# Attention in a macaron block: the maxima of pairs 0 and 1 in one loop on four row groups, pair 0 two steps at a time, projections in single matmuls among the maxima

## The chip, the cores and the metric

The kernel runs on one core of one Trainium2 chip. The core has a matrix engine (TensorE, "PE" in the profile, with its weight loads "PEld"), three engines that work on 128 partitions (VectorE "DVE", ScalarE "ACT", GpSimd "POOL"), and queues for transfers, of which SyncE ("SP") issues those of this kernel. TensorE writes only into PSUM, [...]the other engines empty it. The metric is the device time of one launch in microseconds (us): 3159.78 us, the median of three runs of the kernel before (3156.42 to 3159.99).

## The reference

The block computes, for 2048 tokens x of width 512, three residual stages:

```
x = x + 0.5 * FFN(layernorm(x))
x = x + attention(layernorm(x))      # 16 heads of width 32, causal
x = x + 0.5 * FFN(layernorm(x))      # 4096 hidden, gelu(gate) * up, 4-bit weights dequantized

scores = q @ k.T / sqrt(32);  attn = softmax(scores + causal mask);  out = attn @ v
```

All of it is fp32. Only the middle stage is changed.

## The kernel before, in words

The program is one list of instructions per engine, in the order in which the Python code issues them; each engine works through its list and waits for semaphores where an operand isn't there or a buffer isn't free. So the order of the code is the order of TensorE's queue.

**Tiles.** Tokens are worked on in 16 tiles of 128 (NT) and 4 blocks of 512 (NB). xT[tb] is the normed and transposed input of a block. A projection of q and k (project_qk(u), line 1115) makes 128 rows, four heads, that is two *pairs* of heads: pieces of 4 matmuls (k = 0..3), one for each block and for q and k, into qT and kT, with the bias added on the way out of PSUM. Heads are 32 wide, so a head's q and k are one *row group* of 32 of TensorE's 128 rows; matmuls on different row groups run at once. Pair p uses the row groups 2(p % 2) and 2(p % 2)+1 (quadrant). project_v(half) makes v of 8 heads for two token tiles in a piece, in vals. wqk_sb holds the weights of one u and is refilled by SP.

**Maxima and attention.** For each pair, maxima(p) (lines 1206 to 1243) makes scores with queries on the partitions, q tile by k block, pm; VectorE reduces each to a column (with the mask for a diagonal block, lines 1214 and 1218). There are 40 steps, of two heads each, in blocks g of 4, 8, 12 and 16 steps (STARTS). At the end of a block, finish() splits the maxima into three bf16 pieces on GpSimd, and a few steps later rows() transposes them on TensorE and copies them to mrow (lines 1242 and 1243). attend(p) makes scores anew with keys on the partitions, ps: first a matmul with ones that puts the negated maximum of each query under it (line 1357), then k by q (line 1366); ScalarE takes the exponential into pt (line 1391). A diagonal step masks a 128x128 part first: head 0 with an add on VectorE (line 1381), head 1 by a copy on ScalarE (1384), a select on GpSimd (1385) and an exponential of its own (1393). Then columns() (line 1278) multiplies v and, for the denominators, ones with pt or with the sum of two of them (lines 1413 to 1415). At the end of a block the result is divided: for all pairs but the last through small transfers that spread the denominators over partitions, take the reciprocal and bring it back (flat, packs, back); for the last one directly, a 128x128 reciprocal on VectorE and 32x128 products on GpSimd (chunk).

**Order.** First four pieces of q and k, with the norms of blocks 2 and 3 between them, two steps of norms per maxima step after that. Then maxima(0) alone with 12 whole pieces (the rest of q and k, and v) as fills; then for each pair attend(p) interleaved with maxima(p + 1), so that four row groups are busy in every pass: two with ps, two with pm. The last pair has no maxima ahead and takes two steps at a time; for this the other half of its row groups gets a copy of q and k. Projections of later pairs are fills in the diagonal steps (plan, after_step). Norms are of class Norm (lines 83 to 170): the moments by VectorE's bn_stats and a square root on ScalarE, or, with moments_on_act and power, by sums and squares on ScalarE (lines 99 and 105) and a power on GpSimd (lines 121 to 131).

**Buffers.** PSUM: seven single banks in rotation (ps_one), for pm, ps, rows, projections and transposes, and one for the sums of attention (ps_acc). pt has four buffers, sums two.

## Time and profile before

| what | us |
|---|---|
| median of three runs | 3159.78 |
| the profiled run | 3161.12 |
| its span on the core | 3159.3 |
| first q/k and norms, 1193.9 to 1209.6 | 15.7 |
| maxima of pair 0 alone, 1209.6 to 1291.0 | 81.4 |
| pair 0 with the maxima of pair 1, to 1391.5 | 100.5 |
| pair 1 with the maxima of pair 2, to 1467.6 | 76.1 |
| pair 7, 1959.3 to 2037.7 | 78.4 |

Stages are taken from the first matmul of line 1357 of each pair. In the views, times are from the start of the span; a line of a timeline is start, duration, engine, source line, operation, output and inputs with their shapes, and how many in a row; a bracket gives the idle time of the engine ahead of it and what ended it. A line of the stage table is a stretch, its length, and the busy time and the number of instructions of each engine, then the granted clock of TensorE as a share of the full one, the busy share of the DMA engines and GB/s.

### The profile page before, as it was taken

To read this page: it belongs to the slowest core of one execution; us is meant where nothing else is said; L and a number is where in the kernel's file an instruction comes from. 1 tells how busy PE (TensorE), PEld (TensorE's weight loads), DVE (VectorE), ACT (ScalarE), POOL (GpSimd) and SP (SyncE) were. 2 spreads that over 40 slices of the span, in tenths; PEclk is the share of its full clock that TensorE was granted. 3 is DMA by queue.
4 is the path that set the end of the run, shared out by engine and by line. 5 is a ranking of instruction groups with operands and counts; after the bars stand their busy time and mean duration, and the time that the engine had idled before them with its cause. 6 is when DMAs were issued, how large, how long until landed. Compare 5 with 4: busy or idle time off the path is not lost.

```text
span 3159.3 us, 45153 instructions
## 1 busy us (share of the span) xinstructions
PE 3114.4 (99%) x16592; PEld 2006.8 (64%) x16592; DVE 2055.9 (65%) x3182; ACT 1047.2 (33%) x2070; POOL 1534.8 (49%) x1529
## 2 busy tenths in 40 slices
PE   7999999999999999999999999999999999999998
PEld 4556565656565565444335434478888878888887
DVE  6666666666666655655564566687666777666775
ACT  5111111111111122355453456443333343333332
POOL 3767675857667672456564467522232223223221
PEclk9999999999999999999999999999999999999999
DMA  3223122212122220000000000064444445344441
GB/s 140 79 85 114 67 97 90 97 60 97 64 93 80 83 87 24 5 14 9 12 9 7 29 20 11 1 203 130 124 127 129 125 131 171 116 124 129 130 122 61
DMA packets 261293, 260.21 MB, mean 82 GB/s; under 512 B 21216, under 2 KB 225616, under 8 KB 257104
## 3 DMA queue, kind: packets, MB, share of 16 engines
q1 hardware_dynamic: 261072, 257.33, 25.0%
q8 instruction: 131, 2.15, 0.3%
q14 instruction: 90, 0.74, 0.1%
HBM read 176.28 MB, written 79.92 MB: 81 GB/s over the span
## 4 chain that ended last, share of the span: by engine, by line
PE 93%; DVE 2%; ACT 1%; POOL 1%; issue 1%; DMA 1%; SPq 0%; ACTq 0%; POOLq 0%; DVEq 0%
PE po L438 12%; PE d_f L746 12%; PE pg L339 12%; PE pu L339 12%; PE av L1278 7%; PE pod_f L877 7%; PE pm L1206 6%; PE f_f L746 6%; PE pqk L1122 4%; PE pof_f L877 3%; PE e_f L746 3%; PE ps L1357 2%; PE pv L1139 2%; PE pp L1159 2%; PE poe_f L877 2%; PE ps L1366 1%
## 5 line engine op out<-in xcount | busy, mean ns | idle before, releaser
L1391 ACT ACTIVATE pt<-ps 128x512 f32<-128x512 f32 (+3 forms) x608 | 288.2, 528 | 180.8 <-PE ps L1366 118.5
L1206 PE MATMUL pm<-kT,qT 32*128 32x512 f32 (+3 forms) x1280 | 332.3, 572 | 0.0
L1218 DVE TENSOR_REDUCE parts<-pm 128x1 f32<-128x512 f32 x384 | 246.6, 686 | 129.3 <-PE pm L1206 128.9
L746 PE MATMUL d_f<-ys_f,ring 128*128 128x256 f32 x1216 | 319.8, 384 | 10.1 <-DVE o_f L779 5.8
L1415 POOL TENSOR_TENSOR sum<-pt,pt 128x512 f32<-128x512 f32 (+1 forms) x225 | 265.9, 1202 | 95.2 <-ACT pt L1391 88.1
L1366 PE MATMUL ps<-qT,kT 32*128 32x512 f32 (+3 forms) x1280 | 278.3, 536 | 0.0
L746 PEld LDWEIGHTS d_f<-ys_f,ring 128*128 128x128 f32 x1216 | 226.4, 190 | 58.2 <-DVE o_f L779 21.3
L438 PEld LDWEIGHTS po<-wd,inter 128*128 128x128 f32 x1024 | 194.4, 190 | 77.5 <-issue 55.7
L800 DVE TENSOR_TENSOR o_f<-o_f,o_f 128x1024 f32<-128x1024 f32 x128 | 203.6, 1601 | 61.2 <-ACT o_f L785 56.5
L438 PE MATMUL po<-wd,inter 128*128 128x256 f32 x1024 | 241.1, 379 | 0.0
L339 PE MATMUL pg<-xT_f,w 128*128 128x512 f32 x512 | 240.6, 598 | 0.0
L339 PE MATMUL pu<-xT_f,w 128*128 128x512 f32 x512 | 238.0, 592 | 0.0
L892 POOL TENSOR_TENSOR xq<-xq,d_f 128x512 f32<-128x512 f32 x48 | 63.7, 1326 | 314.6 <-DVE xq L886 229.4
L452 POOL TENSOR_TENSOR xq<-xq,d 128x512 f32<-128x512 f32 x124 | 161.8, 1315 | 92.5 <-DVE xq L446 56.2
L892 POOL TENSOR_TENSOR xq_second<-xq_second,d_f 128x512 f32<-128x512 f32 x45 | 61.6, 1370 | 279.6 <-DVE xq_second L886 210.9
L1278 PE MATMUL av<-pt,vals 128*32 128x256 f32 (+1 forms) x2432 | 191.5, 369 | 2.4 <-ACT both L1300 2.3
L393 POOL TENSOR_TENSOR u<-u,u 128x512 f32<-128x512 f32 x64 | 81.9, 1279 | 211.1 <-ACT u L390 210.4
L438 PEld LDWEIGHTS po<-wd,s 128*128 128x128 f32 x768 | 145.5, 190 | 57.9 <-issue 39.2
L438 PE MATMUL po<-wd,s 128*128 128x256 f32 x768 | 181.4, 379 | 0.0
L339 PE MATMUL pg<-xsum,w 128*128 128x512 f32 x384 | 179.6, 597 | 0.0
L800 POOL TENSOR_TENSOR o_f<-o_f,o_f 128x1024 f32<-128x1024 f32 x44 | 119.2, 2709 | 123.8 <-ACT o_f L785 122.7
L339 PE MATMUL pu<-xsum,w 128*128 128x512 f32 x384 | 177.7, 592 | 0.0
(225 smaller groups left out, 6345.9 us busy)
## 6 DMA issues: line engine op xcount, KB each, us to landing
wd_f<-kept SPq DMA_DIRECT2D x112, 256.0 KB
kept<-wd SPq DMA_DIRECT2D x8, 1792.0 KB
xq<-in_x SPq DMA_DIRECT2D x16, 256.0 KB
pk<-in_gate_codes SPq DMA_DIRECT2D x16, 256.0 KB
sc<-in_gate_scales SPq DMA_DIRECT2D x32, 128.0 KB
pk<-in_up_codes SPq DMA_DIRECT2D x16, 256.0 KB
sc<-in_up_scales SPq DMA_DIRECT2D x32, 128.0 KB
pk<-in_down_codes SPq DMA_DIRECT2D x16, 256.0 KB
```

The lines of the kernel that those rows point to most:

```text
L339: nc.tensor.matmul(ps, lhsT=a[:, j, :], rhs=b[:, j, :], start=(j == 0), stop=(j == 1))
L438: nc.tensor.matmul(ps[:, j, :], lhsT=a[i][:, k, bass.ts(2 * q + j, P)], rhs=b[i][:, k, :], start=(k == 0), stop=(k == 1),)
L452: adder.tensor_tensor(dst, dst, other, ALU.add)
L746: nc.tensor.matmul(ps[:, k, :], lhsT=fa[k][y], rhs=fb[k][y], start=first and k == 0, stop=True, skip_group_check=True,)
L800: sums.append(lambda: eng.tensor_tensor(dst, dst, other, ALU.add))
L877: nc.tensor.matmul(ps[:, j, :], lhsT=a[:, k, bass.ts(2 * q + j, P)], rhs=wd[:, PLACE[i], k, :], start=new and j == k == 0, stop=True, skip ...
L1206: nc.tensor.matmul(ps[a][:, :n], lhsT=q[r, bass.ts(4 * g + i, P)], rhs=k[r, kb * 512 : kb * 512 + n], start=True, stop=True,)
L1218: nc.vector.tensor_reduce(most, scores, AX.X, ALU.max)
L1278: nc.tensor.matmul(dst_, lhsT=lhsT, rhs=rhs, start=kw.get("start", False), stop=True, skip_group_check=True)
L1366: nc.tensor.matmul(ps[a][:, off:], lhsT=k[r, bass.ts(c, P)], rhs=q[r, g * 512 + off : (g + 1) * 512], start=False, stop=True,)
L1391: nc.scalar.activation(pt[:, a, plain[a] :], ps[a][:, plain[a] :], AF.Exp, scale=scale)
L1415: eng.tensor_tensor(s[:, a, off_2:], one[:, a, off_2:], other[:, a, off_2:], ALU.add)
```

## The change

The pairs 0 and 7 form DOUBLE. The maxima of pairs 0 and 1 are made in one loop: each step issues the matmuls of both pairs (four row groups), then the four reductions. Pair 0 is then attended two steps at a time with no maxima beside it, as pair 7 is. Its second row groups read copies of q and k of rows 0 to 63, put into rows 64 to 127 of two tiles by SP, and a second copy of its maxima's rows (mcopy). The projections are cut into units, one matmul of q/k or two of v, issued three per step for three steps and then two per step; they now take in six of eight pieces of the second group of q and k (following), whose weights are fetched in mid-stage (second_group), and the other two are fills of pair 0. Even pieces of these use the bank of ps_acc until attend begins. Only two pieces of q/k go ahead of the maxima, and norms take three steps per maxima step; the norm of block 3 takes its moments on ScalarE and its power on GpSimd. The bias of the first half of v is added on GpSimd after a copy by ScalarE. In pairs 0 and 7 both heads of a diagonal step are masked on VectorE, the division is direct, and VectorE makes one half of the sums. In the diff, whose lines but the first few are all inside attention(), the indentation is cut by twelve.

```diff
...
 STARTS = (0, 4, 12, 24)
+DOUBLE = (0, NPAIR - 1)
 MASKED = -1e30
...
 qT = [qkp.tile([P, S], F32, tag=f"qT{i}", name=f"qT{i}") for i in range(2)]
 kT = [qkp.tile([P, S], F32, tag=f"kT{i}", name=f"kT{i}") for i in range(2)]
-split = [qkp.tile([P, 4, 64], BF16, tag=f"split{i}", name=f"split{i}") for i in range(2)]
+split = [qkp.tile([P, 4, 64], BF16, tag=f"split{i}", name=f"split{i}") for i in range(4)]
 for t in split:
...
 dens = [qkp.tile([P, 256], F32, tag=f"den{i}", name=f"den{i}") for i in range(2)]
...
 ones_f = aw.tile([P, HD], F32, tag="ones_f", name="ones_f")
 nc.gpsimd.memset(ones_f, 1.0)
+copies = [an.tile([P, S], F32, tag="attnT", name=f"copy{i}", bufs=3) for i in range(2)]
+mcopy = [an.tile([P, D], F32, tag="xn", name=f"mcopy{i}").bitcast(BF16) for i in range(2)]
 def normed(nm):
...
     xT.append(x_transposed("a", tb))
-    norms += Norm("a", tb, xT[tb], normed).steps()
-def project_qk(u):
+    norms += Norm("a", tb, xT[tb], normed, moments_on_act=tb == 3, power=tb == 3).steps()
+def joined(pieces):
+    def whole(units):
+        for f in units:
+            f()
+    return [lambda units=units: whole(units) for units in pieces]
+def project_qk(u, bank=None):
     w = wqk_sb
     def piece(tb, j):
-        ps = ps_one.tile([P, 512], F32, tag="one", name=f"pqk_{u}_{j}_{tb}")
-        for k in range(4):
-            nc.tensor.matmul(ps, lhsT=w[:, j, k, :], rhs=xT[tb][:, k, :], start=(k == 0), stop=(k == 3))
-        bias = bqk_sb[:, j, u : u + 1]
-        if j == 0 or u == 0:
-            nc.scalar.activation((qT, kT)[j][u % 2][:, bass.ts(tb, 512)], ps, AF.Identity, bias=bias)
-        else:
-            nc.vector.tensor_scalar(kT[u % 2][:, bass.ts(tb, 512)], ps, bias, None, ALU.add)
-    return [lambda tb=tb, j=j: piece(tb, j) for tb in range(NB) for j in range(2)]
-def project_v(half):
+        ps = []
+        def unit(k):
+            if k == 0:
+                pool, tag = bank(2 * tb + j) if bank else (ps_one, "one")
+                ps.append(pool.tile([P, 512], F32, tag=tag, name=f"pqk_{u}_{j}_{tb}"))
+            nc.tensor.matmul(
+                ps[0], lhsT=w[:, j, k, :], rhs=xT[tb][:, k, :], start=(k == 0), stop=(k == 3)
+            )
+            if k == 3:
+                bias = bqk_sb[:, j, u : u + 1]
+                if j == 0 or u < 2:
+                    nc.scalar.activation(
+                        (qT, kT)[j][u % 2][:, bass.ts(tb, 512)], ps[0], AF.Identity, bias=bias
+                    )
+                else:
+                    nc.vector.tensor_scalar(kT[u % 2][:, bass.ts(tb, 512)], ps[0], bias, None, ALU.add)
+        return [lambda k=k: unit(k) for k in range(4)]
+    return [piece(tb, j) for tb in range(NB) for j in range(2)]
+def project_v(half, bank=None):
     def piece(t2):
-        ps = ps_one.tile([P, 2, 256], F32, tag="one", name=f"pv_{half}_{t2}")
-        for i in range(2):
+        ps = []
+        def unit(n):
+            if n == 0:
+                pool, tag = bank(t2) if bank else (ps_one, "one")
+                ps.append(pool.tile([P, 2, 256], F32, tag=tag, name=f"pv_{half}_{t2}"))
+            i = n // 2
             t = 2 * t2 + i
-            for k in range(4):
+            for k in (2 * (n % 2), 2 * (n % 2) + 1):
                 nc.tensor.matmul(
-                    ps[:, i, :],
+                    ps[0][:, i, :],
                     lhsT=xT[t // 4][:, k, (t % 4) * P : (t % 4 + 1) * P],
...
                 )
-        for i in range(2):
-            nc.vector.tensor_tensor(
-                vals[:, 2 * t2 + i, :, :].rearrange("p h d -> p (h d)"), ps[:, i, :],
-                bv_sb[:, bass.ts(half, 256)], ALU.add,
-            )
-    return [lambda t2=t2: piece(t2) for t2 in range(NT // 2)]
+            if n < 3:
+                return
+            both = vals[:, 2 * t2 : 2 * t2 + 2, :, :].rearrange("p t h d -> p t (h d)")
+            if half == 0:
+                nc.scalar.copy(both, ps[0])
+            for i in range(2):
+                eng, src = (nc.gpsimd, both) if half == 0 else (nc.vector, ps[0])
+                eng.tensor_tensor(both[:, i, :], src[:, i, :], bv_sb[:, bass.ts(half, 256)], ALU.add)
+        return [lambda n=n: unit(n) for n in range(4)]
+    return [piece(t2) for t2 in range(NT // 2)]
 def project_out(u):
...
                 nc.vector.tensor_reduce(nmax, parts, AX.X, ALU.max, negate=True)
-                sp = split[g % 2]
+                sp = split[g % 2 + 2 * (p == 1)]
                 left = nmax
...
                     piece = sp.rearrange("p i (a c) -> p a i c", c=HD)[:, :, :, j]
...
                 def rows(g=g, sp=sp):
-                    halves = (p % 2,) if p + 1 < NPAIR else (0, 1)
+                    halves = (0, 1) if p in DOUBLE else (p % 2,)
                     h = slice(64 * halves[0], 64 * halves[-1] + 64)
...
                             nc.tensor.transpose(row[64 * i : 64 * i + 64, bass.ts(b, P)], sp[:, b, :], identb)
+                    if p == 0:
+                        nc.scalar.copy(mcopy[g // 2][64:, bass.ts(g % 2, 512)], row[64:, :])
+                        h = slice(0, 64)
                     nc.scalar.copy(mrow[h, bass.ts(g, 512)], row[h, :])
...
             rc = dens[g % 2]
-            direct = p == NPAIR - 1
+            direct = p in DOUBLE
             if not direct:
                 flat = store.tile([4, 256], F32, tag=f"flat{g % 2}", name=f"flat_{p}_{g}")
...
         i = 0 if copied else (p // 2) % 2
-        q, k = qT[i], kT[i]
+        q, k = (qT[i], kT[i]) if p or not copied else copies
         def rows_of(a):
-            return slice(HD * a, HD * a + HD) if copied else quadrant(p, a)
+            return quadrant(p + copied, a)
         def maxrows(a):
...
             ps[a] = ps_one.tile([P, 512], F32, tag="one", name=f"ps_{p}_{g}_{c}_{a}")
+            m, at_ = (mrow, g) if p or not copied else (mcopy[g // 2], g % 2)
             nc.tensor.matmul(
...
                 lhsT=ones_b[r.start : r.start + 3, :],
-                rhs=mrow[r.start : r.start + 3, g * 512 + off : (g + 1) * 512],
+                rhs=m[r.start : r.start + 3, at_ * 512 + off : (at_ + 1) * 512],
                 start=True, stop=False,
             )
...
             plain = [off, off]
             if c >= 4 * g:
-                plain[1] = off + P
-                own = pt[:, 1, off : off + P]
-                nc.vector.tensor_tensor(
-                    ps[0][:, off : off + P], ps[0][:, off : off + P], mask_k, ALU.add
-                )
-                nc.scalar.copy(own, ps[1][:, off : off + P])
-                nc.gpsimd.affine_select(
-                    out=own, in_=own, compare_op=ALU.is_ge, fill=MASKED, base=0,
-                    pattern=[[1, P]], channel_multiplier=-1,
-                )
+                for a in range(2 if p in DOUBLE else 1):
+                    own = ps[a][:, off : off + P]
+                    nc.vector.tensor_tensor(own, own, mask_k, ALU.add)
+                if p not in DOUBLE:
+                    plain[1] = off + P
+                    own = pt[:, 1, off : off + P]
+                    nc.scalar.copy(own, ps[1][:, off : off + P])
+                    nc.gpsimd.affine_select(
+                        out=own, in_=own, compare_op=ALU.is_ge, fill=MASKED, base=0,
+                        pattern=[[1, P]], channel_multiplier=-1,
+                    )
             for a in range(2):
...
                     nc.scalar.activation(pt[:, a, plain[a] :], ps[a][:, plain[a] :], AF.Exp, scale=scale)
...
                 else:
                     s = pp.tile([P, 2, 512], F32, tag="sum", name=f"sum_{p}_{g}_{n}", bufs=2)
-                    engines = (nc.vector if p + 1 == NPAIR else nc.gpsimd, nc.gpsimd)
+                    engines = (nc.vector if p in DOUBLE else nc.gpsimd, nc.gpsimd)
                     def add():
                         if off_1 < off_2:
...
         fill[1] -= 1
-qk, v = project_qk(0), project_v(0)
-for piece in qk[:4]:
+begun = []
+def bank(n):
+    return (ps_acc, "acc") if n % 2 == 0 and not begun else (ps_one, "one")
+qk, v, following = project_qk(0, bank), project_v(0, bank), project_qk(1, bank)
+for piece in joined(qk[:2]):
     piece()
...
     del norms[:3]
-fill = qk[4:6] + v[:2] + qk[6:8] + v[2:]
-for n, (matmuls, rest, diagonal) in enumerate(maxima(0)):
+def second_group():
+    nc.sync.dma_start(out=wqk_sb, in_=wqk[1])
+    for src, dst in zip((qT, kT), copies):
+        nc.sync.dma_start(out=dst[64:, :], in_=src[0][:64, :])
+units = []
+for piece in qk[2:6] + v[:2] + qk[6:] + [second_group] + v[2:] + following[:6]:
+    units += piece if isinstance(piece, list) else []
+    if piece is second_group:
+        units.append(lambda f=units.pop(): (f(), second_group()))
+for n, pair in enumerate(zip(maxima(0), maxima(1))):
     for a in range(2):
-        matmuls(a)
+        for matmuls, _, _ in pair:
+            matmuls(a)
     for a in range(2):
-        rest(a, now)
+        for _, rest, _ in pair:
+            rest(a, now)
     now += 1
+    for f in units[: 3 if n < 3 else 2]:
+        f()
+    del units[: 3 if n < 3 else 2]
     run_later(now)
-    for step in norms[:2]:
+    for step in norms[:3]:
         step()
-    del norms[:2]
+    del norms[:3]
     if 12 <= n < 12 + NT:
         nc.gpsimd.tensor_tensor(xs[n - 12], xs[n - 12], bo_sb, ALU.add)
-    if n >= 4 and (n - STARTS[block_of(n)]) % (block_of(n) + 1) == 0:
-        fill.pop(0)()
-assert not fill
+assert not units
+begun.append(True)
 plan = {
-    0: lambda: spread(project_qk(1)),
-    2: lambda: spread(project_qk(2)),
+    0: lambda: [[], following[6], following[7], []],
+    2: lambda: spread(joined(project_qk(2))),
     3: lambda: spread(project_out(0)),
-    4: lambda: spread(project_v(1)[2:] + [lambda: None] * 2, project_qk(3)),
+    4: lambda: spread(joined(project_v(1))[2:] + [lambda: None] * 2, joined(project_qk(3))),
     5: lambda: spread(project_out(1)),
...
 refill = {1: 2, 3: 3}
-nc.sync.dma_start(out=wqk_sb, in_=wqk[1])
 for p in range(NPAIR):
...
         nc.sync.dma_start(out=wqk_sb, in_=wqk[refill[p]])
...
     if p == 4:
-        for piece in project_v(1)[:2]:
+        for piece in joined(project_v(1)[:2]):
             piece()
...
     if p + 1 == NPAIR:
...
                 extra.setdefault(STARTS[3] + after, []).append(step)
-    ahead = maxima(p + 1) if p + 1 < NPAIR else iter(())
+    ahead = iter(()) if p in DOUBLE else maxima(p + 1)
     if p + 2 == NPAIR:
...
     n = 0
-    for steps in attend(p, 2 if p + 1 == NPAIR else 1):
+    for steps in attend(p, 2 if p in DOUBLE else 1):
         if n in STARTS:
...
         other = next(ahead, None)
```

## The prediction

> **What bounds the kernel now.** I read the page's chain of work first, then a table of busy time by stage, TensorE's order in a few stages, and last the waits that end on TensorE. The chain, shares of the span by engine:
>
> ```profile
> PE 93%; DVE 2%; ACT 1%; POOL 1%; issue 1%; DMA 1%; SPq 0%; ACTq 0%; POOLq 0%; DVEq 0%
> ```
>
> Only what lengthens or shortens TensorE's queue counts. Busy time by stage (projections ahead; maxima of pair 0 alone; pair 0; pair 1; pair 7; a stretch of pair 7):
>
> ```profile
> core 0: us, PE busy (x) PEld busy (x) DVE busy (x) ACT busy (x) POOL busy (x), PEclk, DMA share, GB/s
> 1193.90:1209.60 15.70, 15.70 (x50) 7.94 (x48) 7.86 (x21) 7.08 (x12) 2.43 (x10) 1.00 0.23 84
> 1209.60:1291.00 81.40, 80.51 (x351) 45.91 (x352) 49.33 (x130) 10.67 (x18) 22.75 (x31) 1.00 0.02 7
> 1291.00:1391.50 100.50, 100.46 (x931) 40.39 (x926) 56.06 (x142) 50.67 (x119) 53.48 (x82) 1.00 0.04 11
> 1391.50:1467.60 76.10, 75.14 (x911) 30.73 (x907) 52.42 (x138) 47.24 (x117) 56.57 (x86) 1.00 0.03 9
> 1959.30:2037.70 78.40, 73.44 (x772) 33.11 (x772) 45.30 (x86) 44.88 (x115) 41.73 (x67) 0.96 0.01 3
> 2024.50:2031.40 6.90, 5.64 (x45) 2.85 (x48) 2.23 (x6) 4.64 (x15) 2.47 (x6) 0.51 0.01 2
> ```
>
> PE is full in all but pair 7, so covers on other engines are good while they stay below it. TensorE's timeline (start, us, ..., idle before in brackets):
>
> ```profile
> 1268.61 2.84 PE L1206 MATMUL pm<-kT,qT 32*128 32x512 f32 x12
> 1271.38 3.72 PE L1139 MATMUL pv<-wqk_wv,xT_a 128*128 128x256 f32 x16
> 1275.03 3.06 PE L1206 MATMUL pm<-kT,qT 32*128 32x512 f32 x16
> ...
> 1991.11 0.40 PE L1357 MATMUL ps<-wo_bo,ones_b 3*128 3x512 bf16 x4
> 1991.33 1.03 PE L1366 MATMUL ps<-qT,kT 32*128 32x512 f32 x8
> 1993.72 0.39 PE L1357 MATMUL ps<-wo_bo,ones_b 3*128 3x512 bf16 x4
> ...
> 1979.57 0.21 PE L1357 MATMUL ps<-wo_bo,ones_b 3*128 3x128 bf16 x1 [1.20 <-ACT pt L1391]
> 2025.76 0.26 PE L1357 MATMUL ps<-wo_bo,ones_b 3*128 3x128 bf16 x1 [1.99 <-ACT pt L1391]
> ```
>
> Three maxima steps and a piece of v take 6.42 (1268.61 to 1275.03). Each step is two passes of instructions at .43, .86 together; the piece is 16 at .215, 3.44. 3×.86+3.44 = 6.02 leaves .40 for going to the full array and back. Pair 7 puts four row groups through one pass in 1.03, so two more row groups cost next to nothing; a full double step there is 2.62 (1991.11 to 1993.72). VectorE and the chain of a norm (ScalarE, VectorE's reductions, GpSimd):
>
> ```profile
> 1269.77 3.68 DVE L1218 TENSOR_REDUCE parts<-pm 128x1 f32<-128x512 f32 x6
> 31.89 0.61 ACT L99 ACTIVATE sum_f<-xq 128x512 f32<-128x512 f32 x1
> 48.90 0.20 POOL L125 TENSOR_SCALAR rstd_f<-square_f 128x4 f32<-128x4 f32 x1 [0.88 <-ACT sq_f L105]
> ```
>
> A reduction is .60 start to start.
>
> **What the Trainium skill says.** "TensorEngine Tiling (Array Packing)", Key Properties: changing the tiling mode drains TensorE. The .40 per round agrees. Same page, PSUM Bottleneck: tiling speeds TensorE but not the emptying of PSUM; here four reductions (2.40) stay below the 2.97 found below. "TensorE: Matmul & The Clock Gate", Part 1, What's actually happening: an idle window of about 3.4 us halves the clock. The trace has .51 in 2024.5 to 2031.4, after waits of 1.30 and 1.99.
>
> **The change, part by part.**
>
> *To the first score of pair 0.* (1) Only two pieces of q/k now go ahead: 1193.88, with the same 16 instructions and transposes, to 1200.75 and then about 1201.75, since the first maxima wait for kT (a ScalarE bias add, .69). (2) The norm of block 3 goes from VectorE's statistics to ScalarE sums and squares: in the first feed-forward part that chain runs 31.89 to 37.6 = 5.7 on ScalarE, then 48.90 to 50.7 = 1.9 on GpSimd, then the normalize (.9). ScalarE gets to it after its copy of block 2's last transposes, about 1211.2, so the transposes of block 3 can start at 1211.2+5.75+1.95+.9 ≈ 1219.9. TensorE, with three maxima steps and their units, is there at 1213.9. It waits some 6.0 (.6 before); every later maximum and unit is queued behind, and VectorE runs dry. Step 5 then starts at about 1227.1. (3) Steps 5 to 39: maxima 23 full passes ×.86 and three times four diagonals at 2.14 = 26.2; 67 remaining units × .86 (two instructions of .43 for one k of q or k, four of .215 for two matmuls of v) = 57.6; 34 switches ×.39 = 13.3; three joint row blocks of 12 transposes at 1.0 = 3.0. Sum 100.1. First scores at 1327.2, against 1291.0: **+36.2**. The finer units are a loss in themselves: a whole piece paid one .39 for 3.44 of work, a step's two units pay it for 1.72; 34 rounds where 17 would do are +6.6.
>
> A full step is .86+1.72+.39 = 2.97 on TensorE and 4×.60 = 2.40 on VectorE, so the adds of v's bias, now a ScalarE copy (.58) and two GpSimd adds (.73 each, est. from the size), hide: GpSimd has 16 residual adds at 1.26, 16 such adds and 8 splits at 1.45 in 125 us, 43 in all. If that cover went, each would put its length on the ring of PSUM banks. SP gets the refill of wqk and two copies of rows after q/k of block 3; they wait there for the last matmuls and bias adds, nothing else is queued behind them on SP, and their first users come some 25 units (27 us) and the whole stage later; the trace moves 7 GB/s here. Costed at nothing; uncovered it is a few us once.
>
> *Pair 0.* Twelve full double steps at 2.62 = 31.4 and eight diagonal ones at about 2.2 (estimate: widths 512+384 and 256+128 of the same passes) = 17.5, together 48.9. Eight units, two in each of four double steps, at 2×.86+.39 = 2.11: 8.4. The last joint row block 1.0. Stalls: at the start the mask adds queue on VectorE behind the last reductions with no fill to cover, 3.0; 1.5 among the diagonals of block 3, .5 elsewhere; these are judged from pair 7's 1.20 and 1.99. Sum 63.3; with .5 for chance of a slow clock, 63.8 against 100.5: **−36.7**. The direct division (reciprocals on VectorE, 32x128 products on GpSimd) takes eleven small DMAs a block away; none was waited for.
>
> *Clock.* A 6.0 wait may halve the clock for one 3.4 window, about 2.3 lost; even chance: **+1.1**.
>
> *Pair 1*: its own 4 row transposes a block are made already: **−.5**.
>
> *Pair 7*: masks of both heads on VectorE (16 more adds of .2 = 3.2 on an engine with 33 idle), instead of copy, GpSimd select, extra exp. The waits 1.20 and 1.99 end on that extra exp (line 1391 behind line 1385), and the half clock after the second cost about 3. The longer wait gives 1.3 only, as the plain exps of that step are late next; the 1.30 on the last norm stays. I count 1.2+1.3 and 1 of the clock: **−3.5** (−1 to −6.5).
>
> Sum: 36.2−36.7+1.1−.5−3.5 = −3.4. The profiled span 3159.3 becomes 3155.9, its run 3161.1 becomes 3157.7; the median of the runs, 3159.8, becomes 3156.4. I put 3156.5.
>
> *Unknown costs, both ends.* Wait for block 3's norm: 0 (if ScalarE takes its sums earlier) to 8; I take 6.0. Switch per round in the joint stage: .25 to .50 over 34 rounds, −5 to +4; I take .39. Stalls of pair 0: 1 to 9; I take 5.
>
> **Rivals.** *Faster.* The norm's wait is half as long, so the clock stays up, and pair 7 gives 5: −3.4−3−1.1−1.5 = −9, **3151**, down to 3146 with a cheaper switch. For: +11.5 of my sum are waits put in (6.0−.6, 1.1 and 5.0); TensorE's work alone comes out at −14.9. Against: the norm's chain has measured links, and nothing feeds TensorE meanwhile.
>
> *Slower.* VectorE's reductions hold the PSUM ring. A step takes four of seven single banks, and a unit's tile a fifth: the next step's third and fourth scores need the banks of reductions one and two. I find these done 1.76 and 2.36 after the step's start, and the next step starts at 2.97, so no wait; but if each waits for the last reduction (3.0 plus about .6 to free it), a full step is .7 longer, ×24 = +17: **3173**. It decides from a loss of about .4 per full step (24×.4 = 9.6, less 3.4, is +6), that is from reductions over .74 (2.97/4). For: the group mean of the masked and plain ones is .68. Against: .60 is what they keep when they queue.
>
> *It does not do what it says.* The four row groups of two pairs do not overlap: 24×.86+4×2.14 = +29, **3186**. Pair 7's pass of 1.03 speaks against it.
>
> **How the numbers follow.** Near even as summed .46 (own range 3151.5 to 3165); faster rival .32; slower rival .16; no overlap .03; anything else .03, slower. A measurement of this kernel tells about .2%, 6.3 us, from no change: below 3153.5 is faster, above 3166.1 slower. Of the near-even case .07 lies below and .03 above; of the faster one .31 below; the slower ones hold .19, of which .02 stays inside. Faster .38, same .42, slower .20. The range 3146 to 3168 holds .44 of the first, .28 of the second and .06 of the slower ones, .78; both signs are in it.
>
> **What would show it.** Right: first scores of pair 0 near 1327, a wait of about 6 on pt_a before step 3, 2.97 between full maxima steps with PE full, 64 for pair 0, pair 7 near 75 with clock 1.00. Wrong: full steps at 3.3 or more with waits on VectorE at line 1243 (ring); a first score before 1322 (norm hidden); pair 0 over 69 (masks late); pair 7 unchanged, so that its waits were of the norms and not of the select.

## The result, and the profile after

The changed kernel takes 3155.88 us (median of 20 runs, 3152.12 to 3159.65), the kernel before beside it 3159.39 (20 runs): ratio 0.999, 95% interval 0.9983 to 0.9996. It is faster by 3.5 us, a difference that twenty runs can just tell from nothing, inside the 0.2% that I had called "no change". The forecast was 3156.5.

The chain of work that ended last, of the changed kernel, says that TensorE is still what counts:

```profile
PE 93%; DVE 3%; ACT 1%; issue 1%; POOL 1%; DMA 1%; SPq 0%; ACTq 0%; DVEq 0%; POOLq 0%
```

Busy time by stage of the changed kernel (projections ahead; joint maxima up to the waiting norm; the stretch after that wait; the rest of the joint maxima; pair 0; pair 1; pair 7; a stretch of pair 7):

```profile
core 0: us, PE busy (x) PEld busy (x) DVE busy (x) ACT busy (x) POOL busy (x), PEclk, DMA share, GB/s
1192.20:1199.80 7.60, 7.52 (x21) 3.49 (x20) 4.83 (x13) 2.31 (x4) 2.92 (x12) 1.00 0.47 173
1199.80:1217.80 18.00, 12.37 (x54) 5.85 (x54) 6.51 (x24) 12.11 (x29) 1.42 (x3) 0.96 0.01 1
1217.80:1223.20 5.40, 5.37 (x17) 2.65 (x18) 1.44 (x10) 1.98 (x3) 1.74 (x9) 0.50 0.00 2
1223.20:1327.70 104.50, 104.50 (x540) 50.45 (x539) 80.08 (x192) 19.32 (x32) 35.05 (x54) 1.00 0.06 16
1327.70:1389.50 61.80, 59.28 (x724) 25.81 (x719) 28.17 (x64) 41.06 (x88) 32.62 (x49) 0.97 0.03 10
1389.50:1464.10 74.60, 74.39 (x906) 30.62 (x902) 52.70 (x135) 46.37 (x116) 56.38 (x86) 1.00 0.03 8
1955.70:2031.60 75.90, 74.03 (x776) 33.39 (x776) 47.76 (x103) 39.45 (x88) 36.76 (x51) 0.96 0.01 3
2015.00:2023.00 8.00, 6.25 (x49) 3.02 (x46) 5.37 (x18) 3.82 (x10) 5.22 (x7) 0.72 0.01 3
```

The joint stage's 104.50 are full to the last hundredth, with VectorE at 77% of it. Ahead of them stand 5.6 us without work and 5.4 us at clock 0.50. TensorE's timeline there, and two of its full joint steps:

```profile
1217.83 1.13 PE L156 MATMUL pt_a<-ident,xn_a 128*128 128x128 f32 x4 [5.42 <-ACT xn_a L147]
1218.89 0.81 PE L1243 MATMUL pm<-kT,qT 32*128 32x128 f32 x8
1219.63 3.73 PE L1141 MATMUL pqk<-xT_a,wqk_wv 128*128 128x512 f32 x4
...
1263.67 1.14 PE L1243 MATMUL pm<-kT,qT 32*128 32x512 f32 x8
1264.74 2.00 PE L1170 MATMUL pv<-wqk_wv,xT_a 128*128 128x256 f32 x8
1266.67 1.14 PE L1243 MATMUL pm<-kT,qT 32*128 32x512 f32 x8
```

The bracket names the wait: 5.42 on the normed rows. After it four matmul instructions take 3.73; at full clock they take 1.99 (first experiment below). A full step is 3.00 (1263.67 to 1266.67), with eight score instructions (two passes on four row groups) in the 1.07 ahead of the next matmul.

Where the time went, in the two profiled executions (spans 3159.3 and 3153.6):

| stretch | before | after | difference | forecast |
|---|---|---|---|---|
| start to first projection of attention (code not touched) | 1193.9 | 1192.2 | −1.7 | 0 |
| first projection to first score of pair 0 (forecast with 1.1 for the clock) | 97.1 | 135.5 | +38.3 | +37.3 |
| pair 0 | 100.5 | 61.8 | −38.7 | −36.7 |
| pair 1 | 76.1 | 74.6 | −1.5 | −0.5 |
| pairs 2 to 6 | 491.7 | 491.6 | −0.1 | 0 |
| pair 7, to its last score | 78.7 | 75.9 | −2.8 | −3.5 |
| after it | 1121.3 | 1122.0 | +0.7 | 0 |

The touched stretches sum to −4.7 by differences of unrounded times (forecast −3.4). The other −1.0 is in code that both kernels share. TensorE's waits in pair 7 (us in total, times, longest), the first two lines of the kernel before, the last two of the changed one:

```profile
PE ps L1357 <- ACT pt L1391: 3.4, 3, 2.0
PE pt_f L155 <- DVE xn_f L149: 1.5, 2, 1.3
PE pt_f L156 <- DVE xn_f L150: 1.5, 2, 1.3
PE ps L1398 <- ACT pt L1434: 0.3, 1, 0.3
```

The 3.4 us of waits for exponentials are 0.3; the wait on the last norm, which the change didn't touch, is as it was.

### The profile page after: what moved, and what is told of

The parts are those of the page before. It is cut to its first block, busy times and chain, and to the rows that moved or that the text cites. A ratio compares the mean times of both kernels' runs of the same rounds, so it can differ in the third digit from the quotient of the medians.

```text
span 3153.6 us, 45081 instructions
## 1 busy us (share of the span) xinstructions
PE 3104.2 (98%) x16608; PEld 2002.6 (64%) x16608; DVE 2065.1 (65%) x3207; ACT 1048.1 (33%) x2046; POOL 1523.0 (48%) x1515
## 4 chain that ended last, share of the span: by engine, by line
PE 93%; DVE 3%; ACT 1%; issue 1%; POOL 1%; DMA 1%; SPq 0%; ACTq 0%; DVEq 0%; POOLq 0%
PE po L439 12%; PE d_f L747 12%; PE pu L340 12%; PE pg L340 12%; PE av L1318 7%; PE pod_f L878 7%; PE pm L1243 6%; PE f_f L747 6%; PE pqk L1141 4%; PE pof_f L878 3%; PE e_f L747 3%; PE ps L1398 2%; PE pp L1196 2%; PE pv L1170 2%; PE ps L1407 2%; PE poe_f L878 2%
## 5 line engine op out<-in xcount | busy, mean ns | idle before, releaser
L1458 POOL TENSOR_TENSOR sum<-pt,pt 128x512 f32<-128x512 f32 (+1 forms) x210 | 248.8, 1203 | 124.3 <-ACT pt L1434 96.4
L1243 PE MATMUL pm<-kT,qT 32*128 32x512 f32 (+3 forms) x1280 | 296.9, 577 | 0.3 <-ACT kT L1147 0.3
L1407 PE MATMUL ps<-qT,kT 32*128 32x512 f32 (+3 forms) x1200 | 261.9, 540 | 0.0
```

What stands on the lines that cost most here:

```text
L1243: nc.tensor.matmul(ps[a][:, :n], lhsT=q[r, bass.ts(4 * g + i, P)], rhs=k[r, kb * 512 : kb * 512 + n], start=True, stop=True,)
L1407: nc.tensor.matmul(ps[a][:, off:], lhsT=k[r, bass.ts(c, P)], rhs=q[r, g * 512 + off : (g + 1) * 512], start=False, stop=True,)
L1458: eng.tensor_tensor(s[:, a, off_2:], one[:, a, off_2:], other[:, a, off_2:], ALU.add)
```

## The experiments

All were timed beside the kernel before on the same chip. Ratios are to it.

**Block 3's norm back on VectorE.** The changed kernel, with

```diff
-                norms += Norm("a", tb, xT[tb], normed, moments_on_act=tb == 3, power=tb == 3).steps()
+                norms += Norm("a", tb, xT[tb], normed).steps()
```

> The changed kernel, but the norm of block 3 takes its moments on VectorE and its root on ScalarE again, as the kernel before does. My theory: the wait of 5.4 us of TensorE on the normed rows of block 3 (5.42 ahead of the first pt_a at 1217.8) and the half clock after it come from the chain on ScalarE and GpSimd. So the wait falls to 1 us or less, no half clock follows, and the first score of pair 0 comes 5 to 8 us earlier, 128 to 131 us after the first projection instead of 135.5; the median is 5 to 8 us below that of the changed kernel, some 3149 us or 0.9965 of the kernel before. Rival: VectorE is the scarce engine of this stage, and the statistics delay the first reductions by as much; then the first score moves by less than 2 us and the time stays within 2 us of 3156.

Measured: 3148.71 (3147.72 to 3150.56), ratio 0.9964 (0.9952 to 0.9977). TensorE's timeline at the same place, then the stages (projections ahead, joint maxima, pair 0, pair 7):

```profile
1214.32 0.74 PE L156 MATMUL pt_a<-ident,xn_a 128*128 128x128 f32 x4 [0.62 <-ACT xn_a L147]
1214.99 0.50 PE L1243 MATMUL pm<-kT,qT 32*128 32x128 f32 x8
1215.42 1.99 PE L1141 MATMUL pqk<-xT_a,wqk_wv 128*128 128x512 f32 x4
```

```profile
1193.50:1201.10 7.60, 7.51 (x21) 3.48 (x19) 4.83 (x13) 2.31 (x4) 2.92 (x12) 1.00 0.49 173
1201.10:1321.70 120.60, 119.75 (x608) 57.93 (x609) 91.23 (x236) 28.06 (x47) 36.82 (x62) 1.00 0.05 14
1321.70:1382.10 60.40, 57.88 (x721) 25.47 (x715) 28.39 (x64) 40.86 (x88) 32.59 (x49) 1.00 0.03 10
1948.60:2021.70 73.10, 71.11 (x776) 32.43 (x776) 47.78 (x103) 39.38 (x88) 36.75 (x51) 1.00 0.02 4
```

The wait falls from 5.42 to 0.62, the clock stays at 1.00, and the first score comes 128.2 after the first projection instead of 135.5: 7.3, of which 4.8 is the wait, and the rest, 2.5, goes with the clock. VectorE took the statistics, and TensorE waits no more than 0.9 in the 120.60 of the joint maxima. That is the largest single loss that the runs find in the change, and it has nothing to do with joint maxima. The theory holds; the rival is out.

**Pair 7's masks alone.** The kernel before, with

```diff
-                            plain[1] = off + P
-                            own = pt[:, 1, off : off + P]
-                            nc.vector.tensor_tensor(
-                                ps[0][:, off : off + P], ps[0][:, off : off + P], mask_k, ALU.add
-                            )
+                            for a in range(2 if p + 1 == NPAIR else 1):
+                                own = ps[a][:, off : off + P]
+                                nc.vector.tensor_tensor(own, own, mask_k, ALU.add)
+                            if p + 1 < NPAIR:
...
```

(the copy and the select follow under the last condition).

> The kernel before, with only the masks of pair 7 changed (both heads by an add on VectorE). My theory: pair 7's gain is separate and its own: the waits of TensorE on the separate exponential (3.4 us in three waits) fall below 0.6, pair 7 takes 75.9 instead of 78.7, and the median is 2 to 4 us below the kernel before, 0.9991. Then the joint maxima and pair 0 together are worth only 1 to 2 us. Rival: the whole gain of the change is in the joint part, and pair 7 got shorter because its projections and norms were shifted by it; then this kernel is within 1 us of the kernel before.

Measured: 3156.10 (21 runs), ratio 0.9988 (0.9981 to 0.9994). Pair 7 is 73.1 instead of 78.7. Its waits and its stage:

```profile
PE pt_f L155 <- DVE xn_f L149: 1.5, 2, 1.3
PE ps L1357 <- ACT pt L1392: 0.3, 1, 0.3
```

```profile
1958.10:2031.20 73.10, 71.12 (x776) 32.45 (x776) 47.79 (x103) 39.39 (x88) 36.76 (x51) 1.00 0.01 4
```

The theory holds, and the rival is out. The waits are those of the changed kernel, but here the clock stays at 1.00 where the changed kernel's stage shows 0.96: the 2.8 between 73.1 and 75.9 is clock, not code. By the times this small edit alone is worth what the whole change is (0.9988 and 0.999), so joint maxima and pair 0 in double steps, with the slow norm in them, come to nothing that these times can show.

**Whole pieces instead of units.** The changed kernel, with

```diff
-                for f in units[: 3 if n < 3 else 2]:
-                    f()
-                del units[: 3 if n < 3 else 2]
+                count = 3 if n < 4 else 4 * (n % 2 == 0)
+                for f in units[:count]:
+                    f()
+                del units[:count]
```

> The changed kernel, with whole projections of four units after every second joint step instead of two units after every step. My theory: the change of tiling mode costs TensorE about 0.39 us a round, and 17 rounds of 34 are saved, 6.6 us; eight score tiles in a row do not fit in seven single banks, so 0.3 to 0.5 per two steps is lost to a wait on a reduction; net 1 to 4 us gained, two full steps and a piece taking 5.7 to 5.9 instead of 5.97. Rival 1: the switch is cheap and only looks like 0.39, so nothing is saved and the waits make it 5 us slower or more. Rival 2: banks do not bind, then the full 6.6 us is gained, two steps and a piece in 5.6.

Measured: 3170.02 (3167.98 to 3172.35), ratio 1.0031 (1.0019 to 1.0042), slower than both kernels; the first score comes after 147.2. My number was wrong in sign. TensorE's timeline of two steps and a piece, with VectorE's reductions of them:

```profile
1265.45 3.02 PE L1243 MATMUL pm<-kT,qT 32*128 32x512 f32 x16
1266.61 4.87 DVE L1255 TENSOR_REDUCE parts<-pm 128x1 f32<-128x512 f32 x8 [2.93 <-PE pm L1243]
1268.40 3.72 PE L1170 MATMUL pv<-wqk_wv,xT_a 128*128 128x256 f32 x16
1272.06 2.60 PE L1243 MATMUL pm<-kT,qT 32*128 32x512 f32 x15
```

Sixteen score instructions take 2.95 to the start of the piece where two steps of .86 were due, and no bracket of TensorE shows a wait. A tile of scores takes one bank of PSUM, and the eight tiles of two steps share seven. In the single instructions six of the second step's eight start with their neighbours, at 1266.41 and 1266.84, and the last two alone at 1267.36 and 1267.89, after the first reduction (1266.61 to 1267.30) has freed a bank. That is 0.9 after the neighbours' first pass, so both passes of the late fourth matmul run alone, 1.04 (1267.36 to 1268.40), and the profile counts them as busy. The period is 6.61.

**Whole pieces, eight banks.** As before, and

```diff
+                            eighth = p == 1 and a == 1 and now >= 4 and now % 2 == 0
+                            pool, tag = (ps_acc, "acc") if eighth else (ps_one, "one")
-                            ps[a] = ps_one.tile([P, 512], F32, tag="one", name=f"pm_{p}_{g}_{i}_{kb}_{a}")
+                            ps[a] = pool.tile([P, 512], F32, tag=tag, name=f"pm_{p}_{g}_{i}_{kb}_{a}")
...
-                return (ps_acc, "acc") if n % 2 == 0 and not begun else (ps_one, "one")
+                return (ps_one, "one")
```

> Whole pieces of four units after every second joint step, as in the run before with whole pieces, but with every eighth score tile in the bank of ps_acc, so that eight scores in a row have eight banks, and all pieces in the seven single ones. My theory: what made whole pieces slow is the eighth tile alone, which came late and took a pass of 1.04 for itself; with its own bank two steps and a piece take 5.55 to 5.65 instead of 6.60 (and 5.98 with units), and the first score of pair 0 comes some 128.5 to 130 us after the first projection (135.5 with units, 147.1 with pieces and seven banks): 3149 to 3151. Rival: the bunching of scores leaves VectorE short at the end of each pair of steps, so that the waits move to the next tiles, 6.0 or more and no gain.

Measured: 3156.21 (21 runs), ratio 0.9987 (0.9981 to 0.9994); first score after 135.3. TensorE's timeline of the same place:

```profile
1260.01 2.00 PE L1245 MATMUL pm<-kT,qT 32*128 32x512 f32 x16
1261.94 3.72 PE L1170 MATMUL pv<-wqk_wv,xT_a 128*128 128x256 f32 x16
1265.59 2.00 PE L1245 MATMUL pm<-kT,qT 32*128 32x512 f32 x16
```

The same sixteen instructions are done in 2.00; the period is 5.58 as expected (1260.01 to 1265.59), against 6.61 and against 5.98 with units. So both prices are shown: 1.04 for a group broken in this way, 0.40 for a switch to the full array and back. Only seven of the seventeen periods run so, though. After each row of transposes and in the diagonal steps, where VectorE is behind with its reductions, the groups still break, and the whole gain is given back: it ends at 135.3. The mechanism of my theory held and its sum did not; the rival is right at the ends of the blocks.

**All projections in the single banks.** The changed kernel, with the second half of that diff alone.

> The changed kernel, with all projections of the joint stage in the seven single banks (none in the bank of ps_acc), so that a projection's tile always leaves six banks for two steps' eight score tiles. My theory: with one step between two projections' units, the third and fourth tile of a step need the banks of the first two reductions of the step before, done 1.8 and 2.4 us after its start, and the next step comes after 2.99; so full steps stay at 2.99 and the time within 2 us of the changed kernel's 3155.9. Rival (the one on the slower side in my prediction): the ring is at its limit; then a step's last score comes late, makes a pass of its own (0.86 to 1.0), and the stage is 8 us or more longer.

Measured: 3157.53 (21 runs), ratio 0.9989 (0.9983 to 0.9996). Two full steps on TensorE:

```profile
1266.20 1.14 PE L1243 MATMUL pm<-kT,qT 32*128 32x512 f32 x8
1267.27 2.00 PE L1170 MATMUL pv<-wqk_wv,xT_a 128*128 128x256 f32 x8
1269.19 1.23 PE L1243 MATMUL pm<-kT,qT 32*128 32x512 f32 x8
1270.35 2.00 PE L1170 MATMUL pv<-wqk_wv,xT_a 128*128 128x256 f32 x8
```

Every other step is 3.08 (1269.19 to 1272.27) instead of 2.99. In the single instructions its fourth score starts 0.10 after its neighbours in both passes (1269.30 and 1269.83) and runs beside them: a bank that is only a little late costs about as much as it is late, not two passes. The stage is 1.3 longer (136.8); of that 0.5 may be scatter, since the trace of the run with a normalization moved in pair 7, whose joint stage is the changed kernel's, shows 135.9. So the ring is just long enough in the changed kernel, and one bank fewer begins to tell; it is not at the 8 us of the rival.

**v's bias on VectorE.** The changed kernel, with

```diff
-                        if half == 0:
-                            nc.scalar.copy(both, ps[0])
                         for i in range(2):
-                            eng, src = (nc.gpsimd, both) if half == 0 else (nc.vector, ps[0])
-                            eng.tensor_tensor(both[:, i, :], src[:, i, :], bv_sb[:, bass.ts(half, 256)], ALU.add)
+                            nc.vector.tensor_tensor(both[:, i, :], ps[0][:, i, :], bv_sb[:, bass.ts(half, 256)], ALU.add)
```

> The changed kernel, with the bias of v added by VectorE straight from PSUM again (two adds of 0.42 each after every second step) instead of a copy on ScalarE and two adds on GpSimd. My theory: TensorE bounds the stage and VectorE has 0.57 us free in a full step of 2.97, so 0.42 more per step is hidden: full steps stay at 2.99 to 3.05, the stage is at most 1.5 us longer. Rival: VectorE bounds or nearly bounds it; then each of some 13 steps with v is 0.3 or more longer, 4 us and over, and the adds on GpSimd are what makes the joint stage possible.

Measured: 3156.57 (21 runs), ratio 0.9987 (0.998 to 0.9993). Six full steps, this kernel above, the changed one below:

```profile
1259.74:1277.71 17.97, 17.97 (x97) 10.52 (x97) 15.92 (x30) 0.00 (x0) 5.78 (x5) 1.00 0.36 88
```

```profile
1257.68:1275.65 17.97, 17.97 (x97) 10.51 (x96) 14.78 (x26) 1.76 (x3) 7.79 (x9) 1.00 0.34 88
```

VectorE rises from 14.78 to 15.92 of 17.97, and the steps take the same 17.97. TensorE bounds the stage; moving the bias to ScalarE and GpSimd bought nothing here. (The whole stage is 136.0 against 135.5, within the scatter named above.)

**A fill at the start of pair 0.** The changed kernel, with

```diff
-                0: lambda: [[], following[6], following[7], []],
+                0: lambda: [following[6], [], following[7], []],
```

> The changed kernel, with one of pair 0's two projections moved from the diagonal steps of block 1 to those of block 0. My theory: the first double steps of pair 0 are short of work (waits of 0.21, 0.68 and 0.86 on the last reductions, the masks and the exponentials), so units there lie inside waits: pair 0 is 1 to 2 us shorter (60 instead of 61.8), with up to 0.3 given back in block 1. Rival: the units are queued behind the waiting matmuls, since they come after a step, and only delay the next exponentials' operands; then pair 0 stays at 61.8 within 0.4.

Measured: 3153.66 (15 runs), ratio 0.9978 (0.997 to 0.9986); pair 0 is 60.3 instead of 61.8. Of TensorE's timeline, first the changed kernel, then this one:

```profile
1330.96 0.27 PE L1398 MATMUL ps<-wo_bo,ones_b 3*128 3x256 bf16 x1 [0.68 <-DVE parts L1255]
1332.09 0.21 PE L1398 MATMUL ps<-mcopy,ones_b 3*128 3x128 bf16 x1 [0.86 <-ACT pt L1434]
1332.99 1.93 PE L1318 MATMUL av<-pt,vals 128*32 128x256 f32 x16
```

```profile
1332.69 0.21 PE L1398 MATMUL ps<-mcopy,ones_b 3*128 3x128 bf16 x1 [0.22 <-ACT pt L1434]
1333.33 1.07 PE L1318 MATMUL av<-pt,vals 128*32 128x256 f32 x16
```

The waits at the start fall from 0.68 and 0.86 to 0.22, but 0.71 comes back in block 1, whose cover is gone: TensorE's idle time in pair 0 is 2.0 instead of 2.5. The other 1.0 is clock: after the two waits the changed kernel's sixteen av take 1.93, here 1.07. The total was as expected, its cause only in part. That the fill keeps the clock up fits the other traces: none of the five traces with a fill in block 0 (this run and the last four below) has half clock in pair 0, and six of the seven others with double steps in pair 0 have it, for 3.4 us or more. The exception is the first experiment, with 60.4.

**One normalization of pair 7 on ScalarE.** The changed kernel, with

```diff
-                            "f2", tb, xT_f[tb], lambda nm: an.tile([P, D], F32, tag="xn", name=nm), (), power=True
+                            "f2", tb, xT_f[tb], lambda nm: an.tile([P, D], F32, tag="xn", name=nm), (1,) if tb == 0 else (), power=True
```

> The changed kernel, with one of the four normalizations of the first norm inside pair 7 (line 150) moved from VectorE to ScalarE, which is idle for 4.8 us there. My theory: the wait of TensorE of 1.30 on xn_f, which the change did not touch, comes from VectorE being full (3.9 of 4 us) with statistics ahead of it, and the half clock of about 5 us after it costs 2.5 more; so pair 7 is 2 to 4 us shorter (72 to 74 instead of 75.9) and the median 3152 to 3154. Rival: the half clock there has another cause (the low load of the diagonals and transposes); then only the wait of 1.3 goes, or less.

Measured: 3154.72 (21 runs), ratio 0.9986 (0.998 to 0.9993), not to be told from the changed kernel. TensorE's waits in pair 7, and ScalarE's exponentials that end the longest of them:

```profile
PE ps L1398 <- ACT pt L1434: 1.3, 2, 1.1
PE pt_f L156 <- DVE xn_f L150: 0.2, 1, 0.2
2020.26 1.85 ACT L1434 ACTIVATE pt<-ps 128x512 f32<-128x512 f32 x4 [3.68 <-DVE ps L1423]
```

The wait moved from the norm to the exponentials. These don't wait for ScalarE, which is idle for 3.68 ahead of them, but for the masks (line 1423), and the masks stand on VectorE behind two of the norm's statistics and their aggregation (2018.29 to 2019.98). So VectorE's queue is what holds TensorE here, as the theory said, but moving one normalization off it only changes which of its results is late. Pair 7 shows 74.2 at clock 0.98, with 3.4 us of half clock; four traces without the edit and with the same 3.4 us show 74.6 to 74.7. The gain that was expected is not there.

**Three edits together:** VectorE's norm, that normalization, and pair 0's fills in blocks 0 and 1 (`[following[6], following[7], [], []]`).

> What the runs so far favour, together: the changed kernel with block 3's norm on VectorE again, pair 0's two projections in the diagonal steps of blocks 0 and 1 (instead of 1 and 2), and one normalization of pair 7 on ScalarE. My theory: three separate places on TensorE's queue, so the gains add: 7.3 at the norm, 1.5 to 2.2 in pair 0, 1 to 2 in pair 7, some 3145 us, 0.9955 of the kernel before. Rival: pair 7 has nothing more to give, since its clock stayed full in the run with block 3's norm on VectorE and fell in others with the same code there; then 3147, 0.996.

The same kernel was timed again beside the last one below:

> The run of the three edits together once more, on the same chip as the one with closed pieces, so that the two are compared directly: 3144 to 3146 by my theory, and 2 to 3 us above its neighbour; by the rival it is the faster of the two.

Measured: 3144.62 (5 runs, 3140.62 to 3146.39), ratio 0.9951 (0.9939 to 0.9964), and a second time 3147.88 (4 runs), ratio 0.996 (0.9945 to 0.9975). Pair 0 is 59.1 in both profiles, against 60.4 in the first experiment, as the fills of both blocks lie in waits; pair 7 is 74.2, longer than the 73.1 of the first experiment, which hadn't the edit there, but had no half clock either. So in the profiles two of the three edits count. The times alone don't show the second: their intervals overlap with that of the first experiment (0.9952 to 0.9977), and one lies at the theory's 3145, the other nearer the rival's 3147.

**Whole pieces in full steps only,** on top of these: seven pairs of steps with four units after the second and the eighth tile in the bank of ps_acc.

```diff
+PAIRED = (14, 16, 18, 26, 28, 34, 36)
...
+                            eighth = p == 1 and a == 1 and now - 1 in PAIRED
...
+                count = 3 if n < 3 else 0 if n in PAIRED else 4 if n - 1 in PAIRED else 2
```

> The same, and whole pieces after seven pairs of full maxima steps only (steps 14 to 19, 26 to 29 and 34 to 37), with every eighth score tile of these in the bank of ps_acc; single units after all other steps, with their tiles in the single banks. My theory: whole pieces gain 0.39 per pair of full steps and lost it again only after the row transposes and in diagonal steps, where VectorE is behind; so the seven pairs take 5.58 each instead of 5.98, 2.7 us gained, less about 1 for units that have no bank of ps_acc any more: 1 to 2 us below the run it is built on. Rival: the loss follows the bunching wherever it is; then the seven pairs or the steps after them are longer and nothing or less is gained.

Measured: 3151.80 (3147.16 to 3152.95), ratio 0.9973 (0.9964 to 0.9983), slower than what it is built on; the first score comes after 133.5, and the pairs take 6.61:

```profile
1254.64 3.03 PE L1246 MATMUL pm<-kT,qT 32*128 32x512 f32 x16
1257.60 3.72 PE L1171 MATMUL pv<-wqk_wv,xT_a 128*128 128x256 f32 x16
1261.25 3.03 PE L1246 MATMUL pm<-kT,qT 32*128 32x512 f32 x16
```

That is the rival's result, but a piece was left half done across all pairs (31 units by step 13, and a piece is four), so that its tile held a bank. Hence one more:

```diff
-                count = 3 if n < 3 else 0 if n in PAIRED else 4 if n - 1 in PAIRED else 2
+                count = 3 if n < 3 or n == 13 else 0 if n in PAIRED else 4 if n - 1 in PAIRED else 2
...
-                return (ps_one, "one")
+                return (ps_acc, "acc") if n % 2 == 0 and not begun and now - 2 not in PAIRED else (ps_one, "one")
```

> The run before it with whole pieces in full steps, with one unit more in step 13, so that no piece is half done when two steps go in a row (three of its units were done there, and its tile held a single bank through all seven pairs of steps), and with the bank of ps_acc for even pieces outside those pairs. My theory: the pairs took 6.60 for the lack of that one bank, their last two tiles making a pass of their own; with it back they take 5.58, the first score of pair 0 comes 125 to 127 us after the first projection (128.2 without pieces, 133.2 with the open piece), and the median is 2 to 3 us below the run without pieces, about 3142, 0.9945. Rival: the bunching itself is what costs, and the pairs stay over 6.0, the time at 3148 or above.

Measured: 3146.22 (3144.53 to 3147.00), ratio 0.9954 (0.9942 to 0.9967), beside 3147.88 for the three edits without pieces on the same chip. The timeline of the first and the second pair of steps:

```profile
1249.15 3.03 PE L1246 MATMUL pm<-kT,qT 32*128 32x512 f32 x16
1252.11 3.72 PE L1171 MATMUL pv<-wqk_wv,xT_a 128*128 128x256 f32 x16
1255.77 2.00 PE L1246 MATMUL pm<-kT,qT 32*128 32x512 f32 x16
```

Five of seven pairs now take 5.56 to 5.58; the two right after row transposes still break, at 6.6 and 6.7. The first score comes after 127.5 instead of 128.2. The bank was the cause in the five. The gain of 0.7 in the stage is less than I had written down, since five pairs gain 0.4 each and the two broken ones give back 0.5 to 0.6 each. The two times (intervals overlap) don't tell the kernels apart.

## Why the prediction was right

**The joint stage.** The slow norm was forecast to free its transposes 26.0 us after the first projection; it was 25.6, with TensorE waiting 5.42 (forecast 6.0). Both links behind that came out: 5.76 on ScalarE (forecast 5.75) and 1.58 on GpSimd (1.95). The first experiment shows that this chain is the cause. The clock did halve; I had given it an even chance and 1.1, and it cost 2.5. Its price was put together wrongly: 3.4 us at half clock lose 1.7, not 2.3, and the clock stayed down for 6.8, of which 1.4 fell inside the wait. Steps 5 to 39 took 100.0 us (1227.68 to 1327.68), and the sum said 100.1. The full step was right, 2.99 for 2.97; that rested on the 0.40 per switch, which the run with eight banks confirms by taking it away. That the sums agree to a tenth is luck: a row block costs about 0.7 and not 1.0 (0.9 less for three), and 35 steps that are each 0.02 to 0.03 longer make up for it. That VectorE and the PSUM ring don't bound the stage was argued; the runs with the bias on VectorE and with one bank fewer show it, the second that the margin is thin.

**Pair 0.** The step that was off is the term for stalls: 5 us, against 2.4 of waits measured (1.5 on exponentials, 0.9 on reductions). Judging them from pair 7 was too dear, since two of pair 7's three came from the select, which pair 0 doesn't have. A half clock after the first waits, 1.0 to 1.4 here, absent in the first experiment and wherever a fill stands in block 0, took part of it back, and 0.5 had been put in for that.

**Pair 1** gained 1.5 instead of 0.5. Four of its sixteen row transposes are gone, those of one block and not of each. Beside them, TensorE's wait on the copy of pair 0's or its own sums fell from 0.8 to 0.2; that this comes from the order at the seam is not tested.

**Pair 7.** The cause was named rightly: the masks alone, on the kernel before, give pair 7 all of it. (The line in the brackets, 1391, is that of a plain exponential, which stands on ScalarE behind the separate one of line 1393.) Size 2.8 for 3.5 in this profile, made up differently: the waits gave 3.1 and not 2.5, and the clock, counted at 1, gave nothing, as it halved again. It stays up in some runs and not in others with the same instructions, so a single profile can show 2.8 or 5.6.

**Rivals.** The faster one named the two levers that were real, the norm and the clock, at 4.1 for both with half the wait gone; taking the slow norm out gave 7.3. The slower one is out for the kernel as it is, but its mechanism is real and appears as soon as eight scores follow one another. That row groups of two pairs overlap is plain: eight instructions in two passes.

The near-even outcome is thus three things that cancel: TensorE's work falls, the finer switches and a late norm give it back, and pair 7's small edit, unrelated to the rest, brings the larger part of what is left (2.8 of 4.7 in the profiles). That the median came out 0.6 from the forecast is luck beyond that: the stages missed by +1.0, −2.0, −1.0 and +0.7, and single runs of the changed kernel lie up to 7.5 apart.

## What to carry to other kernels

When an engine's queue is full, look at what is queued at its head while the stage starts: here a norm moved off an engine that had room cost 7.3 us, about what the rearrangement of forty steps saved (0.9964 without it against 0.9988 for the masks alone). Count PSUM banks for the longest run of matmuls that are to share the array, an unfinished tile of another product included. And price a large change by its small riders too, each run alone.

## What the runs showed of the hardware that was not expected

A matmul whose PSUM bank comes after its three neighbours have run takes its passes alone: 1.04 us for two instructions (6.61 against 5.58 per two steps and a piece). One whose bank is 0.10 late runs beside them, and the step is 0.09 longer. The profile shows no idle time for either, since the engine counts as busy; only the length of the group, 3.02 or 1.23 against 2.00 or 1.14, gives it away.

The Trainium skill says that TensorE's clock is halved after an idle window of about 3.4 us ("TensorE: Matmul & The Clock Gate", Part 1, What's actually happening). The wait of 5.42 agrees: the clock fell to 0.50 in its course, and that cost 2.5. But the clock also fell where no wait was longer than 0.9 (pair 0) or 1.3 (pair 7), so here the measurement goes beyond that section. The three stretches of half clock in the attention stage of the changed kernel:

```profile
1216.40:1223.20 6.80, 5.37 (x17) 2.65 (x18) 1.44 (x10) 2.82 (x4) 2.19 (x11) 0.50 0.00 1
1332.40:1335.80 3.40, 3.40 (x32) 1.26 (x28) 1.92 (x6) 1.89 (x7) 1.51 (x4) 0.50 0.00 0
2018.50:2025.30 6.80, 6.67 (x50) 2.99 (x49) 2.55 (x8) 3.39 (x10) 2.02 (x3) 0.50 0.01 2
```

They are 3.4 us or twice that, and their starts lie a whole number of steps of 3.41 us apart (34 and 201). In all fourteen traces half clock starts on such a grid and lasts one to three of its steps, but for the last stretch, which runs into the end of the span; the grid lies differently in each execution. So the same instructions can get none, one or two of these steps: pair 7 as the changed kernel has it got none in two traces, one in four and two in two, and takes from 73.1 to 75.9. That it is the place of the grid which decides fits this, but was not tested, and from how low a load the clock falls can't be read from these traces.
